# TensorE transposes in place of transposing DMAs for the rounded integers and the one-hot rows, and the second pair of a branch later on VectorE

## The chip, the cores and the metric

The kernel runs on one core of one Trainium2 chip, in one launch. The metric is the device time of an execution in microseconds (us); lower is better. A time given for a kernel is the median of several executions. The profile is one execution of its own, taken by the hardware profiler, and its span is counted from its first to its last instruction.

## The reference

The input x has 2 x 2048 tokens of 512 channels. The first part of the computation (a modulated linear layer, a gated recurrence over the tokens and a gated feed-forward layer) gives a new x; it takes some 1380 us of the kernel and is not touched by the change. The second part is what matters here. With LN for a layer norm with its gains g and offsets b, and with gains and offsets that are looked up per token in a table:

```
h = LN(x; pw_g[pathway], pw_b[pathway])        # 500 classes
h = LN(h; cp_g[comp], cp_b[comp])              # 5 classes
t = LN(x; tm_g[time], tm_b[time])              # 5 classes
s = LN(x; ms_g[scale], ms_b[scale])            # 3 classes
m, n, r = x + one vector per sample (three small networks)
cat = concat(w0*h, w1*t, w2*m, w3*n, w4*r, w5*s)
c = LN(silu(cat @ int_W1 + b1) @ int_W2 + b2; int_g, int_be)
q = clip(round(c / scale_per_token), -127, 127)      # integers
out = x + (q @ q_rhs) * scale_per_token * scale_per_column
```

## The kernel before, in words

**Blocks.** The second part works on eight blocks of 512 tokens (NB = 8). A block holds its tokens as four tiles of 128 (J = 4), which are handled as two pairs (PAIRS). Data stand either by channels (128 channels on the partitions, tokens along the row: x2T, tT, mT, hT) or by tokens (128 tokens on the partitions: x2n, ln, h0, o4).

**The loop.** The loop at line 1800 runs over the blocks. Round i runs `up(i)`, the product with int_W1, and then `down2(i)`, the product with int_W2. `up` calls `paired_in_place` (line 176), which forms a 2 x 2 block product from seven half-size products, called steps 0 to 6 here. Each step is 32 matmuls of 128x128 by 128x256 f32 into one PSUM bank: step 0 into ps_h_a, 1 into ps_h_b, 2 and 3 into ps_h_d, 4 into ps_h_a, 5 into ps_h_e, 6 into ps_h_a. VectorE and ScalarE empty the banks between them: `out11` (L1600), `out12` (L1603, reads ps_h_d), `tap` (L1578 `less`, L1580 `k3`, L1582 the copies), `out22` (L1608), `out21` (L1613). `added` (L1594) adds two matmuls of a table by z2T to a bank; the one into ps_h_d behind step 5 must wait until `out12` has read that bank.

**Work hung into the steps.** The dictionary `then` names what is traced behind a step: key n is behind step n, key (n, u) behind the first or second half of it. In a round with a block before and a block after, the kernel hangs in: the last norm of the block before (0), its rounding to integers (1), the product of the first pair of integers with rhs (2) and of the second (3, 0), the preparation `by_tokens` of the next block (3), `rows_by_tokens` (6, 0) and `branch_by_channels` (6).

**Preparation of the next block.** `norm_by_tokens` (line 1443) turns x2T to tokens on TensorE (tr_x), takes the statistics, and builds z1: for each token its one-hot row times the reciprocal standard deviation, split over several bf16 terms and repeated for four groups of 32. z1 is turned to classes by tokens (z1T) by `to_rows` (line 1437), one transposing DMA on SP's queue. `branch_by_tokens` (line 1479) gathers the 500-class gains and offsets by token with indirect DMAs on POOL's queue into pw0 and pw1, and applies them to pair 0 and pair 1 on VectorE (L1502, L1503): h0. In the profile pw0 is named zone_B and pw1 pw. `rows_by_tokens` (line 1508) takes the statistics of pair 1 and builds z2, which `to_rows` turns to z2T in the same way. `branch_by_channels` turns h0 to hT on TensorE (tr_h). `gains` (line 1540) multiplies the turned rows by the tables of gains on TensorE and by x on VectorE: n = 0 makes tT and n = 1 mT from z1T, n = 2 makes hT from z2T. A call of `gains` issues four matmuls for two banks of the pools `tr`.

**Integers.** `int8_values` (line 1676) rounds a pair (qn, in the places q0 and q1, which z1 and z2 use as well) and turns it by a transposing DMA to qT (L1685). `int8_product` (line 1690) multiplies it by the integers of rhs (ps_f, L1657).

**Buffers.** PSUM has two pools of one buffer each for turned data, `tr_A` and `tr_B`, taken in turn by `tr(...)` (line 1342), and `m2_ps` with four banks for everything else. Some places in SBUF bear the names of zones in the profile: zone_A holds x2T of even blocks, o4_0 and q0; zone_C holds x2n of even blocks, o4_1 and z1T; zone_B holds pw0 and the copies k0 to k2.

**What sets the order.** Each engine runs its instructions in one order, which a planner makes from a priority (the order in which the code is traced), the data dependencies and its own estimates of durations. `tc.issue_after(ins)` queues instructions behind one of the same engine. In block 0 the order of TensorE up to the end of step 1 is written out by hand, and the calls hung in are those of `in_first`: the second part of z2 goes by a DMA there, and the first is turned on TensorE by `rows_of_first`. The last block has no next one and ends in `part_norm` and `part_product`, where the integers are already turned on TensorE (trq, L1725).

Of the kernel before, what the change touches and what calls it, by code (L numbers as in the profile page):

```python
# [10 lines left out]
BF = mybir.dt.bfloat16  # L11
# [6 lines left out]
P = 128  # L18
B, L, D, F = 2, 2048, 512, 1536
C = D // P  # L20
# [30 lines left out]
def adaln_attn_ffn(ctx: ExitStack, tc: tile.TileContext, a: dict, out: bass.AP):  # L51
# [1382 lines left out]
        )  # L1434
        return ins

    def to_rows(dst, src):
        nc.sync.dma_start(
            dst.rearrange("p a (j t) -> p (a j) t", t=P),
            src.rearrange("p a j t -> p (a j t)"), transpose=True,  # L1440
        )

    def norm_by_tokens(i, k, behind=()):


        def queued(n):
            return tc.issue_after(behind[n].ins) if behind else nullcontext()

        x2n = k["x2n"] = place(f"x2n{i % 2}", J, D)
        mv = small.tile([P, J, 2], FP, tag="mv", name=f"mv1_{i}", bufs=4)  # L1450
        for q in PAIRS:
            if behind:
                turn[0] = 1
            with queued(q):
                pt = tr(f"tr_x_{i}_{q}")
                for j in (0, 1):
                    for c in range(C):
                        nc.tensor.transpose(
                            pt[:, j, ts(c, P)], k["x2T"][:, c, ts(2 * q + j, P)], ident
                        )  # L1460
            nc.scalar.copy(duo(x2n, q), pt)
            for j in (2 * q, 2 * q + 1):
                stats(mv, j, x2n[:, j, :], f"s1_{i}")
        r = rstd_of(mv, f"r1_{i}")

        z1 = by_tiles("q0", i)
        rows = as_rows(r, mv, f"w1_{i}")
        spread_in_groups(z1[:, 0], i, slice(0, 5), rows[:, 0])
        ins = spread_in_groups(z1[:, 1], i, slice(5, 8), rows[:, 0])
        k["z1T"] = place("z1T", 2, T, dtype=BF)  # L1470
        to_rows(k["z1T"], z1)

        k["ln"] = [place(f"o4_{q}", 2, D) for q in PAIRS]
        with tc.issue_after(ins.ins):
            for j in range(J):
                normed(k["ln"][j // 2][:, j % 2, :], x2n[:, j, :], mv, r, j)
        k["rows"] = rows

    def branch_by_tokens(i, k):


        ln = k["ln"]
        z2 = by_tiles("q1", i)
        of_means = z2[:, 1, :, 3 * R : NR].rearrange("p j (q r) -> p j q r", r=RB - R)
        nc.scalar.copy(
            z2[:, 1, :, 0 : 3 * R].rearrange("p j (n r) -> p j n r", r=R),
            onehot[:, i * J : i * J + J, :].unsqueeze(2).to_broadcast([P, J, 3, R]),
        )

        h0 = k["h0"] = []  # L1490
        mv2 = small.tile([P, J, 2], FP, tag="mv", name=f"mv2_{i}", bufs=4)

        def pair_stats(q):
            for j in (0, 1):
                stats(mv2, 2 * q + j, h0[q][:, j, :], f"s2_{i}")

        for q in PAIRS:
            pw = place(f"pw{q}", 2, 2 * D)
            h0.append(pw[:, :, 0:D])
            for j in (0, 1):  # L1500
                gather(i * J + 2 * q + j, pw[:, j, :])
            nc.vector.tensor_mul(h0[q], ln[q], h0[q])  # L1502
            nc.vector.tensor_add(h0[q], h0[q], pw[:, :, D : 2 * D])  # L1503
            if not q:
                pair_stats(0)
        k["rest"] = z2, of_means, mv2, pair_stats

    def rows_by_tokens(i, k):
        z2, of_means, mv2, pair_stats = k["rest"]
        rows = k["rows"]  # L1510
        pair_stats(1)
        spread(of_means[:, :, :, 0:8], i, slice(0, 8), rows[:, 1])
        r = rstd_of(mv2, f"r2_{i}")
        rows = as_rows(r, mv2, f"w2_{i}")
        spread_in_groups(z2[:, 0], i, slice(0, 5), rows[:, 0])
        last = spread(of_means[:, :, :, 8:], i, slice(0, 5), rows[:, 1])
        k["z2T"] = place(f"z2T{i % 2}", 2, T, dtype=BF)
        if i:
            to_rows(k["z2T"], z2)
        else:  # L1520
            k["z2"] = z2
            to_rows(k["z2T"][:, 1:2], z2[:, 1:2])
        return last

    def rows_of_first():

        pt = m2_ps.tile([P, D], BF, tag="mm", name="tr_z2")
        for j in range(J):
            nc.tensor.transpose(pt[:, ts(j, P)], k["z2"][:, 0, j, :], identb)
        nc.scalar.copy(k["z2T"][:, 0, :], pt)  # L1530

    def by_tokens(i, k):
        norm_by_tokens(i, k)
# [27 lines left out]
    def up(i, k, then):  # L1561
        h1 = h1s[i] = block("h1")
        h_a, h_b = slice(0, H), slice(H, T)

        first, second = (k["x2T"], block("mT")), (block("tT"), block("hT", i))

        def banks(n):
            return m2_ps.tile([P, 2, H], FP, tag="mm", name=f"ps_h1_{i}_{n}").rearrange(
                "p u t -> u p t"
            )  # L1570

        def both(ps):
            return ps.rearrange("u p t -> p u t")

        def tap(n, ps, less):
            t = place(f"k{ {1: 0, 4: 1, 2: 2, 5: 1, 3: 1, 6: 2}[n]}", 2, H)
            if n == 5:
                nc.vector.tensor_sub(t, ps, less)  # L1578
            elif n == 3:
                held["k3"] = nc.vector.tensor_add(t, both(ps), less)  # L1580
            else:
                nc.scalar.copy(t, both(ps))  # L1582
            return t

        def silu(o, half, src):
            nc.scalar.activation(
                h1[:, o, half], src, AF.Silu, bias=col("L0_cond2_int_b1", o)
            )

        def added(n, ps):  # L1590

            o, half = {1: (0, h_a), 2: (0, h_b), 3: (2, h_b), 4: (2, h_a)}[n]
            for u in (0, 1):
                nc.tensor.matmul(  # L1594
                    ps[u], tables[:NR, 3, ts(o + u, P)], k["z2T"][:NR, 1, half],
                    start=False, stop=(n != 2), skip_group_check=True,
                )

        def out11(ps, kept):
            nc.vector.tensor_add(h1[:, 0:2, h_a], both(ps), kept)  # L1600

        def out12(ps, kept):
            nc.vector.tensor_add(h1[:, 0:2, h_b], both(ps), kept)  # L1603
            for o in (0, 1):
                silu(o, slice(0, T), h1[:, o, :])

        def out22(ps, kept):
            nc.vector.tensor_add(h1[:, 2:4, h_b], both(ps), kept)  # L1608
            for o in (2, 3):
                silu(o, h_b, h1[:, o, h_b])  # L1610

        def out21(ps, kept):
            nc.vector.tensor_add(h1[:, 2:4, h_a], both(ps), kept)  # L1613
            for o in (2, 3):
                silu(o, h_a, h1[:, o, h_a])

        paired_in_place(
            w_int, *([t[:, :, h] for t in q] for h in (h_a, h_b) for q in (first, second)),
            banks, tap, out11, out12, out21, out22, then, added, True, None if i else behind_branch,
        )  # L1620

    def down2(i, nxt):
# [4 lines left out]
        for q in (1, 0):  # L1627
            for j in (2 * q, 2 * q + 1):
# [1 line left out]
                    gains(i + 1, nxt, (2, 3, 0).index(j))  # L1630
                ps = m2_ps.tile([P, D], FP, tag="mm", name=f"ps_o_{i}_{j}")
                for c in range(C):
                    nc.tensor.matmul(  # L1633
                        ps, h1[:, c, ts(j, P)], w2[:, c, :], start=(c == 0), stop=(c == C - 1)
                    )
                t = o4[q][:, j % 2, :]
                nc.vector.tensor_add(t, ps, b2_bc)
                stats(mv, j, t, f"s3_{i}")
# [37 lines left out]
    def int8_values(i, qs, q):  # L1676

        t = o4s[i][q]
        for j in (0, 1):
# [2 lines left out]
        qn = place(f"q{q}", 2, D, dtype=BF)  # L1682
        rounded(qn, t)
        nc.vector.tensor_scalar(qn, qn, -127.0, None, ALU.max)
        nc.sync.dma_start(  # L1685
            place(f"qT{q}", 2, D, dtype=BF).rearrange("p j (c t) -> p (j c) t", t=P),
            qn.rearrange("p j d -> p (j d)"), transpose=True,
        )

    def int8_product(i, qs, x2n, q, behind):  # L1690

# [42 lines left out]
    with tc.high_priority():  # L1734
        k = load(0)
        norm_by_tokens(0, k, (ends[4], mids[5]))
        branch_by_tokens(0, k)
        branch_rows = rows_by_tokens(0, k)

    first_block = ExitStack()  # L1740
# [43 lines left out]
    def behind_branch(n):  # L1784
# [3 lines left out]
    in_first = {  # L1788
        (0, 1, 0): steps(class_bias, lambda: branch_by_channels(0, k)),
        (0, 0, 1): times,  # L1790
        (0, 1, 1): rows_of_first,
        (1, 0, 0): lambda: gains(0, k, 2),
        1: first_block.close,
    }
    def behind_k3(i, k):
        with tc.issue_after(held["k3"].ins):
            rows_by_tokens(i, k)

    last = None
    for i in range(NB):  # L1800
        nxt = load(i + 1) if i + 1 < NB else None
        then = {} if last else in_first
        if last:
            qs = []
            then[0] = lambda: qs.append(last_norm(i - 1))
            then[1] = lambda: [int8_values(i - 1, qs[0], q) for q in PAIRS]
            then[2] = lambda: int8_product(i - 1, qs[0], last["x2n"], 0, held["ins"])
            then[3, 0] = lambda: int8_product(i - 1, qs[0], last["x2n"], 1, held["ins"])
        if nxt:
            then[3] = lambda: by_tokens(i + 1, nxt)  # L1810
            then[6, 0] = lambda: behind_k3(i + 1, nxt)
            then[6] = lambda: branch_by_channels(i + 1, nxt)
        else:

# [83 lines left out]
```

## Time and profile before

| | us |
|---|---|
| median of 3 executions | 1993.96 (1993.28 to 1995.19) |
| the profiled execution | 1991.8 |
| its span | 1990.0 |
| TensorE busy (99%) | 1972.5 |
| VectorE busy (59%) | 1180.4 |
| ScalarE busy (33%) | 658.4 |
| GpSimd busy (7%) | 146.4 |
| mean granted clock of TensorE | 0.997 |

In the profile PE is TensorE's matmuls, PEld its weight loads, DVE is VectorE, ACT is ScalarE, POOL is GpSimd, and SPq is the DMA queue that SyncE issues to. A line such as "DVE h L1603" means the instruction of line 1603 that writes tile h. Matmuls overlap each other, so the time of a group of them is longer than the distance between the starts by the length of one. Transposing DMAs of the span: eight for z1T (named zone_C), eight for z2T, and seven for each qT, all on SP's queue. TensorE has transposes of f32 tiles (tr_x, tr_h) and, in two places, of bf16 tiles: four of z2 in block 0 (tr_z, L1529) and sixteen of integers in the tail (trq, L1725).

### The profile page before, as it was taken

What the parts mean: (1) busy time and instruction counts of PE and PEld (TensorE: products, weight loads), DVE (VectorE), ACT (ScalarE), POOL (GpSimd) and SP (SyncE); (2) the same over time, 40 slices, a digit from 0 to 9 for tenths busy, and PEclk for the clock granted to TensorE, in tenths of its full rate; (3) what the DMA queues carried; (4) which work ended last, traced back from release to release, by engine and by line L of the source; (5) the groups of instructions that cost most, each with busy time, mean ns of one, the idle gap of its engine ahead of it and who ended that gap; (6) DMA issues with size and microseconds to landing.
All of it is one profiled execution on the core that took longest, in us unless ns stands there. A gap on an engine that the chain in (4) does not pass through costs nothing.

```text
span 1990.0 us, 16593 instructions
## 1 busy us (share of the span) xinstructions
PE 1972.5 (99%) x6060; PEld 1054.8 (53%) x6068; DVE 1180.4 (59%) x1907; ACT 658.4 (33%) x889; POOL 146.4 (7%) x123
## 2 busy tenths in 40 slices
PE   9999999999999999999999999999999999999997
PEld 5444444444444444444444444444867867877774
DVE  6667666666633324324224564646788888788775
ACT  4557777777522222222221100001213213212302
POOL 0241000000400000000010000025000000000000
PEclk9999999999999999999999999999999999999999
DMA  6661212121511212111335666453322222222110
GB/s 220 204 201 53 89 59 95 53 95 43 159 47 66 89 42 82 56 42 53 101 100 170 209 232 235 156 170 127 121 69 85 59 72 82 65 73 74 43 32 22
DMA packets 115774, 201.36 MB, mean 101 GB/s; under 512 B 37728, under 2 KB 66034, under 8 KB 111596
## 3 DMA queue, kind: packets, MB, share of 16 engines
q1 hardware_dynamic: 111028, 183.49, 28.2%
q0 software_dynamic: 4608, 16.78, 2.4%
q8 instruction: 48, 0.79, 0.2%
q14 instruction: 34, 0.28, 0.0%
q10 hardware_dynamic: 56, 0.03, 0.0%
HBM read 133.59 MB, written 58.83 MB: 97 GB/s over the span
## 4 chain that ended last, share of the span: by engine, by line
PE 93%; DVE 5%; ACT 0%; DMA 0%; issue 0%; SPq 0%; DVEq 0%
PE up_a L134 17%; PE rec_a L134 11%; PE dn_a L134 8%; PE up_d L134 8%; PE ps_h_a L134 6%; PE ps_h_d L134 6%; PE rec_d L134 6%; PE ps_o L1633 5%; PE dn_d L134 4%; PE up_b L134 4%; PE ps_h_b L134 3%; PE y_a L134 3%; PE rec_b L134 3%; PE dn_b L134 2%; PE y_d L134 1%; PE ps_f L1657 1%
## 5 line engine op out<-in xcount | busy, mean ns | idle before, releaser
L134 PE MATMUL up_a<-h,w_up 128*128 128x512 f32 x384 | 172.6, 592 | 0.0
L134 PE MATMUL dn_a<-op,w_dn 128*128 128x512 f32 x384 | 168.9, 599 | 0.0
L821 DVE SCALAR_TENSOR_TENSOR prod<-up_d,cols,k 128x512 f32<-128x512 f32 x48 | 36.0, 750 | 199.5 <-ACT k L304 199.5
L304 ACT COPY k<-up_a 128x512 f32<-128x512 f32 x144 | 84.0, 584 | 196.8 <-PE up_a L134 196.7
L801 ACT ACTIVATE gate<-gate,cols 128x512 f32<-128x512 f32 x96 | 68.8, 721 | 215.3 <-DVE gate L800 214.2
L134 PE MATMUL up_a<-h2T,w_up 128*128 128x512 f32 x288 | 129.5, 593 | 0.0
L134 PEld LDWEIGHTS up_a<-h,w_up 128*128 128x128 f32 x384 | 73.1, 190 | 91.7 <-issue 89.3
L134 PEld LDWEIGHTS dn_a<-op,w_dn 128*128 128x128 f32 x384 | 73.0, 192 | 90.2 <-issue 89.7
L134 PE MATMUL rec_a<-h,w_rec 128*128 128x512 f32 x256 | 115.1, 592 | 0.0
L134 PE MATMUL rec_a<-hT,w_rec 128*128 128x512 f32 x256 | 115.1, 592 | 0.0
L1633 PE MATMUL ps_o<-int_w,h 128*128 128x512 f32 x224 | 103.6, 606 | 0.0
L134 PEld LDWEIGHTS up_a<-h2T,w_up 128*128 128x128 f32 x288 | 54.8, 190 | 68.8 <-issue 68.8
L134 PE MATMUL up_b<-h,w_up 128*128 128x512 f32 x192 | 86.3, 592 | 0.0
L134 PE MATMUL up_d<-h,w_up 128*128 128x512 f32 x192 | 86.3, 593 | 0.0
L134 PE MATMUL dn_d<-op,w_dn 128*128 128x512 f32 x192 | 83.7, 594 | 0.0
L134 PEld LDWEIGHTS rec_a<-hT,w_rec 128*128 128x128 f32 x256 | 48.7, 190 | 61.2 <-issue 61.2
L134 PEld LDWEIGHTS rec_a<-h,w_rec 128*128 128x128 f32 x256 | 48.7, 190 | 61.2 <-issue 60.7
L304 ACT COPY k<-rec_a 128x512 f32<-128x512 f32 x96 | 55.6, 579 | 71.5 <-PE rec_a L134 70.0
L800 DVE TENSOR_TENSOR gate<-up_b,k 128x512 f32<-128x512 f32 x48 | 32.9, 690 | 72.1 <-PE up_b L134 71.0
L134 PE MATMUL up_d<-h2T,w_up 128*128 128x512 f32 x144 | 65.2, 593 | 0.0
L1633 PEld LDWEIGHTS ps_o<-int_w,h 128*128 128x128 f32 x224 | 40.3, 190 | 46.5 <-issue 46.5
L222 DVE TENSOR_TENSOR op<-op,op 128x3072 f32<-128x3072 f32 x16 | 55.2, 3448 | 16.2 <-PE dn_d L134 9.3
(408 smaller groups left out, 3403.2 us busy)
## 6 DMA issues: line engine op xcount, KB each, us to landing
pp_d<-prod SPq DMA_DIRECT2D x48, 512.0 KB
op<-pp_d SPq DMA_DIRECT2D x16, 1536.0 KB
y_d<-y SPq DMA_DIRECT2D x16, 512.0 KB
h<-y_d SPq DMA_DIRECT2D x4, 2048.0 KB
yr<-y_d SPq DMA_DIRECT2D x16, 512.0 KB
hs_d<-yr SPq DMA_DIRECT2D x16, 512.0 KB
h<-hs_d SPq DMA_DIRECT2D x4, 2048.0 KB
op<-in_xT SPq DMA_DIRECT2D x32, 256.0 KB
```

What stands on the lines that cost most here:

```text
L134: ins = nc.tensor.matmul(ps, ws[k // 2][:, slot, k % 2, ts(u, P)], xs[k], start=(first and k == 0), stop=(last and k == n - 1), skip_group ...
L222: nc.vector.tensor_sub(t, p, q)
L304: nc.scalar.copy(t, ps)
L800: nc.vector.tensor_add(gate[u][:, half], ps, kept)
L801: nc.scalar.activation(gate[u][:, half], gate[u][:, half], AF.Gelu, bias=col("L0_attn_mlp_gate_b", fs[u]),)
L821: nc.vector.scalar_tensor_tensor(prod[u][:, b_], ps, col("L0_attn_mlp_fc_b", fs[u]), kept, ALU.add, ALU.add)
L1633: nc.tensor.matmul(ps, h1[:, c, ts(j, P)], w2[:, c, :], start=(c == 0), stop=(c == C - 1))
L1657: nc.tensor.matmul(ps, qT[:, ts(c, P)], rq[:, c, :], start=(c == 0), stop=(c == C - 1))
```

## The change

z1, z2 and the integers of the blocks 0 to 6 are turned by TensorE, through a bank of `tr` and a copy by ScalarE, and no transposing DMA is left. z1 of the next block is turned behind step 4, z2 behind the matmuls of the third tile (j = 2, the first that `down2` works on), the first pair of integers behind the first half of step 2 and the second behind step 2. In block 0 z2 is turned in two parts through banks of `m2_ps`. The multiplication and addition of pair 1 in `branch_by_tokens` become a function `pair(q)` of their own, which for pair 1 is traced behind step 5 and queued on VectorE behind `less`; in block 0 it is called right after `branch_by_tokens`.

```diff
-    def to_rows(dst, src):
-        nc.sync.dma_start(
-            dst.rearrange("p a (j t) -> p (a j) t", t=P),
-            src.rearrange("p a j t -> p (a j t)"), transpose=True,
-        )
+    def to_rows(dst, src, pt):
+        for n in range(dst.shape[1]):
+            for j in range(J):
+                nc.tensor.transpose(pt[:, n, ts(j, P)], src[:, n, j, :], identb)
+        nc.scalar.copy(dst, pt)
...
-        to_rows(k["z1T"], z1)
+        k["z1"] = z1
...
+        def pair(q):
             nc.vector.tensor_mul(h0[q], ln[q], h0[q])
-            nc.vector.tensor_add(h0[q], h0[q], pw[:, :, D : 2 * D])
-            if not q:
-                pair_stats(0)
+            nc.vector.tensor_add(h0[q], h0[q], place(f"pw{q}", 2, 2 * D)[:, :, D : 2 * D])
+
+        pair(0)
+        pair_stats(0)
+        k["pair"] = pair
...
-        if i:
-            to_rows(k["z2T"], z2)
-        else:
-            k["z2"] = z2
-            to_rows(k["z2T"][:, 1:2], z2[:, 1:2])
+        k["z2"] = z2
...
+    def rows_of_first(n):
+
+        pt = m2_ps.tile([P, 1, D], BF, tag="mm", name=f"tr_z2_0_{n}")
+        to_rows(k["z2T"][:, n : n + 1], k["z2"][:, n : n + 1], pt)
+
+    def rows_of(n, i, k):
+        to_rows(k[f"z{n}T"], k[f"z{n}"], tr(f"tr_z{n}_{i}", BF))
...
-                nc.vector.tensor_sub(t, ps, less)
+                held["less"] = nc.vector.tensor_sub(t, ps, less)
...
+                if nxt and j == 2:
+                    with tc.issue_after(ins.ins):
+                        rows_of(2, i + 1, nxt)
...
-        nc.sync.dma_start(
-            place(f"qT{q}", 2, D, dtype=BF).rearrange("p j (c t) -> p (j c) t", t=P),
-            qn.rearrange("p j d -> p (j d)"), transpose=True,
-        )
+
+    def int8_rows(i, q, behind):
+
+        qn, pt = place(f"q{q}", 2, D, dtype=BF), tr(f"trq_{i}_{q}", BF)
+        with tc.issue_after(behind.ins):
+            for j in (0, 1):
+                for c in range(C):
+                    nc.tensor.transpose(pt[:, j, ts(c, P)], qn[:, j, ts(c, P)], identb)
+        nc.scalar.copy(place(f"qT{q}", 2, D, dtype=BF), pt)
...
         norm_by_tokens(0, k, (ends[4], mids[5]))
+        rows_of(1, 0, k)
         branch_by_tokens(0, k)
+        k["pair"](1)
...
-        (0, 1, 1): rows_of_first,
+        (0, 1, 1): lambda: rows_of_first(0),
+        (1, 1, 0): lambda: rows_of_first(1),
...
-            then[2] = lambda: int8_product(i - 1, qs[0], last["x2n"], 0, held["ins"])
+            then[2, 0] = lambda: int8_rows(i - 1, 0, held["ins"])
+            then[2] = lambda: (
+                int8_rows(i - 1, 1, held["ins"]),
+                int8_product(i - 1, qs[0], last["x2n"], 0, held["ins"]),
+            )
...
-            then[6, 0] = lambda: behind_k3(i + 1, nxt)
+            then[5] = lambda: behind("less", nxt["pair"], 1)
+            then[6, 0] = lambda: behind("k3", rows_by_tokens, i + 1, nxt)
+            then[4] = lambda: behind("ins", rows_of, 1, i + 1, nxt)
```

`behind(name, f, *args)` calls f inside `tc.issue_after(held[name].ins)`.

More of the change, by code (lines that the diff above doesn't have):

```diff
@@ L1517, in rows_by_tokens @@
         k["z2T"] = place(f"z2T{i % 2}", 2, T, dtype=BF)
-        if i:
-            to_rows(k["z2T"], z2)
-        else:
-            k["z2"] = z2
-            to_rows(k["z2T"][:, 1:2], z2[:, 1:2])
-        return last
[L1525 to L1530, printed above, removed]
+        k["z2"] = z2
+        return last
+    def rows_of_first(n):
[3 more added lines that the diff above has]
+        to_rows(k[f"z{n}T"], k[f"z{n}"], tr(f"tr_z{n}_{i}", BF))
     def by_tokens(i, k):
@@ L1632, in down2 @@
                 for c in range(C):
-                    nc.tensor.matmul(
+                    ins = nc.tensor.matmul(
                         ps, h1[:, c, ts(j, P)], w2[:, c, :], start=(c == 0), stop=(c == C - 1)
                     )
+                if nxt and j == 2:
+                    with tc.issue_after(ins.ins):
+                        rows_of(2, i + 1, nxt)
                 t = o4[q][:, j % 2, :]
@@ L1794, in adaln_attn_ffn, with behind @@
     }
-    def behind_k3(i, k):
-        with tc.issue_after(held["k3"].ins):
-            rows_by_tokens(i, k)
+    def behind(name, f, *args):
+        with tc.issue_after(held[name].ins):
+            f(*args)
     last = None
```

## The prediction, made before the changed kernel was run

> **What bounds the kernel now.** I read the page first, then TensorE's waits, then the order of time in one block of the last stage.
>
> From the page (busy us, share of the span):
> ```profile
> span 1990.0 us, 16593 instructions
> PE 1972.5 (99%) x6060; PEld 1054.8 (53%) x6068; DVE 1180.4 (59%) x1907; ACT 658.4 (33%) x889; POOL 146.4 (7%) x123
> ```
> TensorE (PE) works through the whole span; VectorE and ScalarE have room. A busy PE is not always a useful one, so the next question is where it waits. From TensorE's waits (total us, times, longest):
> ```profile
> PE ps_h_d L1594 <- DVE h L1603: 3.6, 7, 0.6
> PE ps_h_b L134 <- DVE tT L1555: 0.9, 1, 0.9
> PE tr_z L1529 <- ACT q L1432: 0.4, 1, 0.4
> ```
> Nowhere in this view does PE wait for a transposing DMA: the waits that are not here lie at the start or in the tail, which the change leaves alone. One wait comes back seven times, once in every block that prepares a next one. Its cause is in VectorE's order of time of such a block (start us, us):
> ```profile
> 1504.65 1.22 DVE L1502 TENSOR_TENSOR zone_B<-zone_A,zone_B 128x1024 f32<-128x1024 f32 x1
> 1505.79 1.22 DVE L1502 TENSOR_TENSOR pw<-zone_C,pw 128x1024 f32<-128x1024 f32 x1
> 1506.92 1.21 DVE L1503 TENSOR_TENSOR zone_B<-zone_B 128x1024 f32<-128x1024 f32 x1
> 1508.06 1.22 DVE L1503 TENSOR_TENSOR pw<-pw 128x1024 f32<-128x1024 f32 x1
> 1509.19 1.28 DVE L1348 BATCH_NORM_STATS2 s_st<-zone_B 128x6 f32<-128x512 f32 x2
> ...
> 1510.47 0.65 DVE L1603 TENSOR_TENSOR h<-ps_h_d,zone_B 128x512 f32<-128x512 f32 x1
> ```
> L1603 is `out12`: it empties the bank ps_h_d, which PE adds to next. Ahead of it stand both pairs of the first branch, zone_B (pair 0) and pw (pair 1). VectorE has idled before this run and is busy without a gap from 1501 on, so its queue, not data, makes L1603 late. PE sees (start us, us, then idle before):
> ```profile
> 1508.78 1.89 PE L134 MATMUL ps_h_e<-mT,w_int 128*128 128x256 f32 x8
> 1511.17 0.38 PE L1594 MATMUL ps_h_d<-z2T,tables 108*128 108x256 bf16 x2 [0.51 <-DVE h L1603]
> ```
> So the block's period, 73.0 us (ps_h_a begins at 1463.30 and 1536.32 on the chain), is PE's work plus 0.5.
>
> **What the change adds: transposes on PE.** The counts are from the code. Per prepared block: 8 for z1, 8 for z2, and, for the integers of the block before, 2 x 8. That is 32 in each of seven rounds (224), and 12 for block 0 (8 of z1, the 4 of z2 that a DMA did). Same operation, same type and shape, back to back, in the tail and once in block 0:
> ```profile
> 1972.83 0.61 PE L1725 MATMUL trq<-identb,zone_B 128*128 128x128 bf16 x8
> 1398.47 0.38 PE L1529 MATMUL tr_z<-identb,q 128*128 128x128 bf16 x4 [0.38 <-ACT q L1432]
> ```
> One lasts 0.219 us, but eight take 0.61: the pitch is (0.61 - 0.22) / 7 = 0.0555 us. PE has nothing idle to hide them in, so they count in full: 224 x 0.0555 = **12.4 us**, and 12 x 0.0555 = **0.7 us** for block 0. Not pipelined they would cost 236 x 0.219 = 51.7 us; the row shows them pipelined, so I take the pitch.
>
> The Trainium skill speaks against the change here: "TensorE: Matmul & The Clock Gate", Part 4, PE-mode transpose, gives about 275 ns for one 128x128 bf16 transpose inside a kernel and 390 ns alone. By that, an estimate from the page, 236 would take 64.9 us and the kernel would come near 2060 us. This trace's pitch of 0.0555 us differs from it five times over, and the measurement decides.
>
> A seam behind them: f32 transposes of the same 128 columns come every 0.109 us (ten from 1495.60, the next matmul at 1496.69), so an f32 weight load seems to need that much, where a 0.055 us transpose before it covers half. Two groups a round are followed by f32 work (the first integers in the middle of step 2, z1 before step 5): 14 x 0.054 = **0.8 us**, bounds nothing and 14 x 0.3 = 4.2 (the seam behind a `gain` group, below).
>
> **ScalarE's copies** cost four of 1024 bf16 columns per round. No row shows one: 0.569 us for 512 bf16 (L1530) and 1.01 us for 1024 f32 (L1374) bound it; I take 1.0, so 4 us more of a 73 us round, in an engine that is busy 33%. Each stands ahead of its user by this order: the first integers turn at about 1480.8 (values rounded at 1478.7), copied by 1482.3, used at 1484.5; z1's last copy of rows ends at 1503.57, and step 4 ends on PE at 1503.6, so its transposes begin without a wait, though with almost no slack; its z1T is used at 1520.4. The copies that empty ps_h_a (1503.86) and ps_h_d (1486.22) share the queue with them. If one such copy were put ahead of an emptying one, PE would wait up to 1 us.
>
> **The two banks `tr`.** z2 turns behind the matmuls of the second half's first tile, at about 1525, in a bank that the next `gains` needs: its second pair now waits for the copy, to about 1526.4. PE's order is made by the planner, which already splits such a group:
> ```profile
> 1520.43 0.39 PE L1551 MATMUL gain<-zone_C,tables 30*128 30x512 bf16 x2
> 1520.76 1.13 PE L1633 MATMUL ps_o<-int_w,h 128*128 128x512 f32 x2
> 1521.81 0.39 PE L1551 MATMUL gain<-zone_C,tables 30*128 30x512 bf16 x2
> 1522.13 2.84 PE L1633 MATMUL ps_o<-int_w,h 128*128 128x512 f32 x6
> 1524.91 0.40 PE L1551 MATMUL gain<-zone_C,tables 18*128 18x512 bf16 x4
> 1525.23 3.70 PE L1633 MATMUL ps_o<-int_w,h 128*128 128x512 f32 x8
> ```
> The first `gains` stands in two groups of 2 because its second bank is still being emptied; the second stands in one of 4. From that group at 1524.91 to the one at 1528.87 are 3.96 us, and eight ps_o at 0.432 (dn_a: 36 in 15.54) make 3.46: a group costs 0.50 us, of 2 or of 4, as the four run side by side. I expect the group of 4 to be split: 7 x 0.50 = **3.5 us** (bounds 0 and a PE that waits in order, 7 x 1.0 = 7).
>
> **What it removes.** With pair 1 behind `less`, the two operations of pair 1 (1.14 each) leave VectorE's queue ahead of L1603, which ends at 1508.9 instead of 1511.1; step 5 now ends at about 1511.1 with z1's 0.44. The 0.51 goes with 2.2 us to spare: **-3.6 us** for seven. Pair 1 then runs from 1509.5 to 1511.8, in VectorE's time before k3 (1511.89), and tr_h reads it only at 1519.2; statistics of pair 1 stay behind k3. What is late next is PE itself. Block 0's own pair keeps its place, and no gather moves on POOL's queue in the loop (each waits for tr_h).
>
> The transposing DMAs leave SP's queue: eight of z1, eight of z2, fourteen of the integers, 1.23 us of issue each. Behind them SP issues the load of x2T (1508.97, which waits for PE) and the outputs, none of which PE waits for. Worth nothing. In block 0, z1's transposes stand in the last matmuls of the stage before (about 1375 to 1383); z1T is read at 1383.70, and the bank is free by then: nothing beyond the 0.44 counted.
>
> **Sum:** 12.4 + 0.7 + 0.8 + 3.5 - 3.6 = **+13.8 us**. The profiled execution took 1991.8 us (span 1990.0 and 1.8 around it), so 2005.6; the median shown is 1993.96, 2.2 above it, and against that I predict **2007.8 us**, 0.7% slower. About 0.2% (4 us) is what a measurement of this kernel can tell from no change.
>
> **Rivals.**
> - *No split* (28%): the second `gains` stays in one group without a wait. The gaps between groups on PE would be as before. +10.3: 2004.3 us.
> - *A new wait* (16%): z1's slack is under 0.2 us, and four more copies stand in ScalarE's queue; one wait of 1 us a round on PE adds 7: 2014.8 us. Against it: ScalarE idles for over 2 us ahead of most of these places.
> - *The wait stays* (8%): if the planner keeps pair 1 ahead of L1603, or the emptying copy of ps_h_a comes late behind z1's, the 3.6 are not gained: 2011.4 us. This is the case that the change does not do what it says.
> - *Not slower* (8%): the groups of `gains` merge. There are four a round at 0.50; if the new order issues two fewer in each of seven rounds, 7.0 come back on top of the case without a split: +3.3, 1997.3 us, within the 4 us. It decides from two merged groups a round on; one alone leaves +6.8. For it: two of the groups are parts of one `gains`. Against: the copies of tr_h that split them are unchanged. A gain beyond that would need PE work that vanishes, and none does.
>
> **How the numbers follow.** The forecast has 40%, the rivals 28, 16, 8 and 8. PE's 13.1 us of transposes are certain within a few tenths, so all but the last are slower by over 0.2%. The low end, 2000.7, is the case without a split, less 0.8 of seams and 2.8 for waits in block 0 and before step 3 that transposes may fill; the high end is 2014.8, the new wait. Outside lie the last rival and part of the new wait. Slower 0.90, within 0.2% 0.06, faster 0.04 (half of the last rival, and all that I overlook).
>
> **What would show it.** In the profile after: 7 waits of ps_h_d for L1603 gone; trq, tr_z1, tr_z2 groups of 8 at 0.055 pitch; the block's period 73.0 + 1.8 = 74.8 us; the second `gains` as 2 + 2; no wait over 0.1 us at a transpose. A pitch near 0.1, or a wait for ScalarE at a `tr` bank or at ps_h_a, would make the prediction too low; a period under 74 us would make it too high.

## The result and the profile after

The changed kernel takes 2007.65 us (median of 4, 2006.97 to 2009.90) beside 1993.62 us of the kernel before: a ratio of 1.0073, with a 95% interval of 1.0056 to 1.0090. It is slower by about 14 us; the forecast was 2007.8 us.

The profiled execution took 2007.17 us, with this head of its page:

```profile
span 2005.4 us, 17000 instructions
PE 1990.9 (99%) x6296; PEld 1069.6 (53%) x6304; DVE 1179.0 (59%) x1907; ACT 687.2 (34%) x919; POOL 146.2 (7%) x123
```

The 236 further matmuls on PE are the transposes. PE is as full as before, at a longer span; VectorE's work is the same, and ScalarE has 29 us more, the copies. The span grew by 15.4 us, of which 1.6 are not the change's: on PE, the last transposes of x ahead of every changed instruction begin 1.56 us later than in the profile before (1368.84 and 1367.28). What is left, 13.8 us, is the change.

TensorE's waits after (total us, times, longest) no longer hold the seven for L1603 (L1604 now). Of block 0's waits one grew from 0.4 to 0.6 and one came twice instead of once:

```profile
PE ps_h_b L134 <- DVE tT L1556: 1.5, 2, 0.9
...
PE tr_z L1440 <- ACT q L1432: 0.6, 1, 0.6
```

VectorE's order of time in the same round (start us, us) shows `out12` (L1604) moved ahead of both the addition of pair 0 and all of pair 1 (pw); it ends at 1511.27, 4.5 us before PE needs its bank at 1515.80:

```profile
1509.44 1.22 DVE L1504 TENSOR_TENSOR zone_B<-zone_A,zone_B 128x1024 f32<-128x1024 f32 x1
1510.58 0.69 DVE L1604 TENSOR_TENSOR h<-ps_h_d,zone_B 128x512 f32<-128x512 f32 x1
...
1514.19 1.19 DVE L1504 TENSOR_TENSOR pw<-zone_C,pw 128x1024 f32<-128x1024 f32 x1
```

And PE's order, with the three kinds of transposes (trq for the integers, tr_z from zone_A for z1, tr_z from q for z2) and the group that broke:

```profile
1484.47 0.61 PE L1696 MATMUL trq<-identb,zone_A 128*128 128x128 bf16 x8
1484.91 1.95 PE L134 MATMUL ps_h_d<-tT,w_int 128*128 128x256 f32 x8
1486.69 1.89 PE L134 MATMUL ps_h_d<-hT,w_int 128*128 128x256 f32 x8
...
1508.39 0.61 PE L1440 MATMUL tr_z<-identb,zone_A 128*128 128x128 bf16 x8
...
1514.07 1.89 PE L134 MATMUL ps_h_e<-mT,w_int 128*128 128x256 f32 x8
1515.80 0.38 PE L1595 MATMUL ps_h_d<-z2T,tables 108*128 108x256 bf16 x2
...
1529.44 0.61 PE L1440 MATMUL tr_z<-identb,q 128*128 128x128 bf16 x8
1529.99 0.39 PE L1552 MATMUL gain<-zone_C,tables 18*128 18x512 bf16 x2
1530.31 1.13 PE L1634 MATMUL ps_o<-int_w,h 128*128 128x512 f32 x2
1531.36 0.39 PE L1552 MATMUL gain<-zone_C,tables 18*128 18x512 bf16 x2
```

Eight transposes begin at 1484.47 and the next matmul at 1484.91: they cost the stream 0.44 us, whatever the 0.61 of their row says. From 1514.07 to 1515.80 are 1.73 us, eight matmuls at 0.216: ps_h_d is waited for no more. The second `gains` (18 rows) stands as 2 + 2 with two matmuls of ps_o between, where it was one group of 4.

A number to compare kernels by is the period: the distance between the starts of step 0 (the first matmul into ps_h_a) in consecutive rounds. Over the six full rounds of a trace (those with a block before and a block after) it repeats within 0.02 us, where medians scatter by 1 us. It was 73.03 us and is 74.78 us, 1.74 more before rounding. The experiments are read by it.

### The profile page after: what moved, and what is told of

It is laid out like the page before. It is cut to its first block, busy times and chain, and to the rows that moved or that the text cites. A ratio compares the mean times of both kernels' runs of the same rounds, so it can differ in the third digit from the quotient of the medians.

```text
span 2005.4 us, 17000 instructions
## 1 busy us (share of the span) xinstructions
PE 1990.9 (99%) x6296; PEld 1069.6 (53%) x6304; DVE 1179.0 (59%) x1907; ACT 687.2 (34%) x919; POOL 146.2 (7%) x123
## 4 chain that ended last, share of the span: by engine, by line
PE 99%; DVE 1%; ACT 0%; issue 0%
PE up_a L134 16%; PE rec_a L134 11%; PE dn_a L134 8%; PE up_d L134 8%; PE ps_h_a L134 8%; PE ps_h_d L134 6%; PE rec_d L134 6%; PE ps_o L1634 5%; PE dn_d L134 4%; PE up_b L134 4%; PE ps_h_e L134 3%; PE y_a L134 3%; PE rec_b L134 3%; PE ps_h_b L134 3%; PE dn_b L134 2%; PE y_d L134 1%
```

## The experiments

The theory behind all of them: the stream of PE is the time. Each term of the sum is a piece of that stream, and nothing off PE counts unless PE waits for it.

**1. Pair 1 alone.** The kernel before, with the one edit:

```diff
+        pair(0)
+        pair_stats(0)
+        k["pair"] = pair
...
+            then[5] = lambda: behind("less", nxt["pair"], 1)
```

> The kernel before with the second pair alone moved: queued on VectorE behind `less`, all transposes by DMA as before. The theory (TensorE's stream of work is the time, and every term of the sum is a piece of it): the seven waits for L1603 go, and each was worth its idle 0.51 us plus the 0.16 by which a matmul's modelled end (0.38 us) lies behind the next start at full pitch (0.216): 7 x 0.67 = -4.7 us, a period of 72.36 us, about 1989 beside 1993.6 us. As the prediction sized it: -3.6, about 1990. Rival (pair 1 only moves the wait to k3 or to tr_h): within 1 us of before.

Measured: 1991.02 us beside 1992.55, ratio 0.9988 (0.9979 to 0.9997); the period is 72.65, so 0.39 us less a round, not 0.67 (and not the 0.51 of the prediction). The wait for L1603 is gone, and a new one of 0.3 stands seven times. PE, then ScalarE, in that round:

```profile
1521.03 0.38 PE L1598 MATMUL ps_h_a<-z2T,tables 108*128 108x256 bf16 x2
1521.70 0.39 PE L1555 MATMUL gain<-zone_C,tables 30*128 30x512 bf16 x2 [0.29 <-ACT hT L1374]
```
```profile
1520.25 0.49 ACT L1432 COPY q<-q 128x360 bf16<-128x360 bf16 x1 [2.48 <-DVE q L1423]
1520.65 1.92 ACT L1374 COPY hT<-tr_h 128x1024 f32<-128x1024 f32 x2
```

ScalarE's queue holds the copy of z2 ahead of the copies of tr_h. PE reaches this place earlier than before, the chain that makes z2 does not, and `gains` finds its bank still full. In the kernel before, the copies of tr_h began with ScalarE waiting for PE:

```profile
1519.37 1.93 ACT L1374 COPY hT<-tr_h 128x1024 f32<-128x1024 f32 x2 [0.17 <-PE tr_h L1371]
```

The rival had the kind right, not the size: 0.28 of the 0.67 came back as a wait for the copies of tr_h.

**2. The transposes without the move.** The changed kernel, with pair 1 back ahead of `out12` (its two later calls go):

```diff
         pair(0)
         pair_stats(0)
-        k["pair"] = pair
+        pair(1)
...
```

> The changed kernel with pair 1 back in its old place ahead of L1603: all transposes on TensorE, nothing moved on VectorE. The theory: z1's transposes put 0.50 us (8 x 0.0555 and a seam of 0.054) between the start of VectorE's chain and the place where TensorE needs ps_h_d, so they lie in the old wait, and only 0.17 of it is left: +1.2 us against the changed kernel, 2008.9. Then most of what the move gains alone is gained by z1's transposes already, and the move itself is worth little in the changed kernel. Rival (the terms add, as the prediction summed them): the whole wait is back, +3.6 to +4.7, 2011.3 to 2012.4 us.

Measured: 2006.87 us beside 1992.55, ratio 1.0071 (1.0057 to 1.0085), which the medians can't tell from the changed kernel's 1.0073. The period can: 74.95, 0.17 above 74.78, as the theory had it. In the changed kernel the move is worth 0.17 us a round and not 0.5.

**3. The integers alone.** The kernel before with `int8_rows` and its two calls in place of the DMA at L1685, nothing else.

> The kernel before with only the integers turned on TensorE; z1 and z2 by DMA, pair 1 in its old place. The theory: seven rounds of 16 transposes at 0.0555 and one seam of 0.054 behind the first group: 7 x 0.94 = +6.6 us, the wait for L1603 unchanged at 0.51, about 2000.2 us. Rival (no split groups of gains in the account, the 13.8 us lie in dearer transposes, about 0.075 us each): 112 x 0.075 = +8.4, about 2002 us. Rival (the waits of the integers on a DMA cost TensorE something): less than +6.

Measured: 2000.14 us beside 1992.55, ratio 1.0035 (1.0022 to 1.0047); period 73.99, +0.96 (expected 0.94). The waits for L1603 stand as they were (3.7 us in 7). Taking fourteen transposing DMAs away gave PE no measurable time back.

**4. z2 through another bank.** The changed kernel, with

```diff
-        to_rows(k[f"z{n}T"], k[f"z{n}"], tr(f"tr_z{n}_{i}", BF))
+        name = f"tr_z{n}_{i}"
+        pt = tr(name, BF) if n == 1 else m2_ps.tile([P, 2, D], BF, tag="mm", name=name)
+        to_rows(k[f"z{n}T"], k[f"z{n}"], pt)
```

> The changed kernel with z2 turned through a bank of m2_ps instead of tr, so that the second gains need not wait for the copy of z2 and stand in one group of four. The theory: seven groups fewer at 0.515 us, -3.6 us against the changed kernel, a period of 74.26 us, about 2004.0. Rival (the time lies in the transposes, and a split group costs nothing): 2007.6, the period as it was at 74.78 us.

Measured: 2003.14 us beside 1992.55, ratio 1.0052 (1.0039 to 1.0066); period 74.26, 0.52 below the changed kernel. PE's order of time shows why:

```profile
1528.09 0.61 PE L1440 MATMUL tr_z<-identb,q 128*128 128x128 bf16 x8
1528.64 0.40 PE L1554 MATMUL gain<-zone_C,tables 18*128 18x512 bf16 x4
1528.96 3.70 PE L1636 MATMUL ps_o<-int_w,h 128*128 128x512 f32 x8
```

The bank was the cause of the split, and a split costs 0.52 us.

**5. The integers twice.** The changed kernel, each transpose of the integers issued twice into the same place (`for j in (0, 0, 1, 1)`).

> The changed kernel with each transpose of the integers issued twice into the same bank (112 more on TensorE, the same values). The theory: a further transpose costs its pitch and nothing else, 16 x 0.0555 = 0.89 us a round: a period of 75.67 us beside 74.78, +6.2 us, about 2013.5. Rival (a transpose costs what a single one lasts, 0.219, or more): +24.5 us and up.

Measured: 2013.98 us beside 1992.84, ratio 1.0106 (1.0090 to 1.0121); period 75.67, +0.89, the expected number. The group of sixteen:

```profile
1484.88 1.06 PE L1696 MATMUL trq<-identb,zone_A 128*128 128x128 bf16 x16
1485.77 1.95 PE L134 MATMUL ps_h_d<-tT,w_int 128*128 128x256 f32 x8
```

Sixteen in 0.89 us of the stream: 0.056 each, also in a longer run. This settles the price of a transpose in a row here. It is the pitch, not the 0.219 that one lasts. For one in a kernel the Trainium skill ("TensorE: Matmul & The Clock Gate", Part 4, PE-mode transpose) gives about 0.275, which the prediction weighed and which is not the price here either.

**6. z1 alone.** The kernel before with z1 turned on TensorE behind step 4; z2, the integers and pair 1 as before.

> The kernel before with only z1 turned on TensorE; z2 and the integers by DMA, pair 1 in its old place. The theory: the 0.50 us of z1's transposes lie in the wait for L1603, so the period stays at 73.03 us and the wait shrinks from a loss of 0.67 to 0.17; only block 0's 0.44 is paid, about +0.4 us. Rival (the terms add): 7 x 0.50 + 0.44 = +3.9 us, a period of 73.53, the wait unchanged.

Measured: 1994.39 us beside 1992.84, ratio 1.0003 (0.9994 to 1.0012), no difference; period 73.04. Eight transposes a round cost nothing here, because they stand where PE waited. PE at `out12`'s bank:

```profile
1509.48 1.89 PE L134 MATMUL ps_h_e<-mT,w_int 128*128 128x256 f32 x8
1511.38 0.38 PE L1603 MATMUL ps_h_d<-z2T,tables 108*128 108x256 bf16 x2
```

From 1509.48 to 1511.38 are 1.90 us for eight matmuls of 0.216 (1.73): 0.17 are lost to a wait, though the row shows no idle time. In the kernel before it was 1511.17 - 1508.78 = 2.39, so 0.66 were lost, where the row says 0.51.

**7 to 9. Toward a faster kernel.** The prices above point at the kernel before: keep the DMAs, drop the wait, and keep the groups whole. First, experiment 1 with the first `gains` behind the second product of ps_o (four matmuls in the profile):

```diff
-                if nxt and j in (2, 3, 0):
+                if nxt and j in (3, 0):
...
+                    if nxt and j == 2 and c == 1:
+                        with tc.issue_after(ins.ins):
+                            gains(i + 1, nxt, 0)
```

> The kernel before with pair 1 moved (as in the first experiment) and the first gains queued behind the second matmul of ps_o, so that both its banks are free and its four matmuls stand in one group. The theory: a group fewer is worth 0.515 us a round, and the new wait of the first experiment (gain for the copy of tr_h, 0.28 us) goes with it, since two matmuls of ps_o stand ahead: a period of 73.03 - 0.67 - 0.515 = 71.85 us, 7 x 1.18 = -8.3 us, about 1985 us. Rival (splitting a group costs nothing, only the wait goes): 72.36, about 1988. Rival (tT comes late for the next block): no better than the first experiment's 72.65.

Measured: 1988.08 us beside 1992.84, ratio 0.9975 (0.9964 to 0.9985); period 72.37, not 71.85. The first `gains` was whole and its wait gone (0.28), but now the second broke:

```profile
1523.16 0.39 PE L1555 MATMUL gain<-zone_C,tables 30*128 30x512 bf16 x4
1523.48 1.98 PE L1637 MATMUL ps_o<-int_w,h 128*128 128x512 f32 x4
1525.40 0.39 PE L1555 MATMUL gain<-zone_C,tables 18*128 18x512 bf16 x2
1526.00 0.39 PE L1555 MATMUL gain<-zone_C,tables 18*128 18x512 bf16 x2 [0.21 <-issue]
```

Between the two calls there are only 1.9 us of ps_o, and VectorE reads the first call's second bank until 1525.95. The theory's number failed. The first rival's number (72.36) was met, but not by its reason: splitting costs, and the split came back elsewhere.

Next, the product of the first integers behind the table matmuls of step 2 (`added`, n = 2), so that PE has work while ScalarE empties ps_h_d:

```diff
+            if n == 2 and "first" in held:
+                held.pop("first")(ins)
...
-            then[2] = lambda: int8_product(i - 1, qs[0], last["x2n"], 0, held["ins"])
+            held["first"] = lambda ins: int8_product(i - 1, qs[0], last["x2n"], 0, ins)
```

> The kernel of the last experiment, and the product of the first pair of integers queued behind the table matmuls of step 2 instead of ahead of them. TensorE then has 1.73 us of work while ScalarE empties ps_h_d (0.58), where now six transposes of x (0.65) leave it 0.285 us short ahead of step 3. The theory: 0.285 us a round less, a period of 71.56 us, about 1983 us. Rival (the integers' product or the transposes of x come late elsewhere, so that the wait turns up again before step 4 or at the norm): the period stays at 71.85 or more.

Measured: 1985.66 us beside 1992.84, ratio 0.9966 (0.9954 to 0.9978); period 72.09, 0.29 below experiment 7, the expected step (0.285) from another start. The product, of whose eight matmuls the profile kept seven, now stands between the two, and step 3 begins eight pitches of 0.216 behind its start, without a loss:

```profile
1481.66 0.38 PE L1598 MATMUL ps_h_d<-z2T,tables 108*128 108x256 bf16 x2
1481.88 1.89 PE L1666 MATMUL ps_f<-rq,qT 128*128 128x512 bf16 x7
1483.61 1.89 PE L134 MATMUL ps_h_d<-x2T,w_int 128*128 128x256 f32 x8
```

Last, all three `gains` behind the second product of their tile:

```diff
-                if nxt and j in (3, 0):
-                    gains(i + 1, nxt, (2, 3, 0).index(j))
...
-                    if nxt and j == 2 and c == 1:
+                    if nxt and j in (2, 3, 0) and c == 1:
                         with tc.issue_after(ins.ins):
-                            gains(i + 1, nxt, 0)
+                            gains(i + 1, nxt, (2, 3, 0).index(j))
```

> The kernel of the last experiment with all three gains of a round queued behind the second product of their tile of ps_o. In the two experiments before, the first gains became whole, but the second then found its second bank still being read by VectorE and broke in two, with a loss of 0.59 us between its halves (1525.246 to 1525.840), so nothing was won by the group. The theory (a group costs about 0.5 us wherever it stands): with 1.8 us of ps_o more between the first and the second, no group breaks, a period of 72.09 - 0.59 = 71.50 us, 7 x 0.59 = 4.1 us less, about 1981.5 us. Rival (VectorE's products of the gains set the pace, and the break moves to the third gains or to the next block's first step): 72.0 or more.

Measured: 1982.88 us beside 1993.05, ratio 0.9949 (0.9936 to 0.9963); period 71.49, as expected. It is the fastest kernel of the study, 10 us under the one before and 25 under the changed one. Its groups are whole:

```profile
1522.43 0.40 PE L1555 MATMUL gain<-zone_C,tables 30*128 30x512 bf16 x4
1522.75 3.70 PE L1637 MATMUL ps_o<-int_w,h 128*128 128x512 f32 x8
1526.38 0.39 PE L1555 MATMUL gain<-zone_C,tables 18*128 18x512 bf16 x4
```

## Why the prediction was right, point by point

The account of the 13.8 us, from the places of PE's matmuls in both traces: block 0's z1 0.50; from block 0's first `gains` to the next step 0, 1.78; six full rounds at 1.743, 10.46; the round without a next block 0.95; the tail 0.13. Against the prediction, us a round:

| term | predicted | measured | from |
|---|---|---|---|
| 32 transposes | 1.78 | 1.78 | 16 more: +0.89 (experiment 5) |
| seams to f32 work | 0.11 | 0.11 | 1486.69 - 1484.91 = 1.78 for eight at 0.216, twice |
| a group more of `gains` | 0.50 | 0.52 | 74.78 - 74.26 (4) |
| the wait for `out12` | -0.52 | -0.67 | 0.50 by z1 alone (6), 0.17 by the move on top (2) |
| sum | 1.87 | 1.74 | periods |

- **PE bounds, and transposes count in full**, except where they fill a wait: shown (3, 5, 6). The transposing DMAs were worth nothing to PE (3, 6). The pitch, not the length of one, is the price.
- **The split group**: shown by name and by size (4).
- **The wait**: the sum was right that it goes; its size and its cause were not. It was undersized, 0.51 for 0.67, because the idle time of a row starts at the modelled end of the matmul before, 0.38 after its start, where a next one could start after 0.216. And it was credited to the move on VectorE. z1's transposes alone fill 0.50 of it, so either may be called free: the move gains 0.39 by itself and 0.17 beside z1's transposes. The prediction saw that step 5 ends 0.44 later and used it only as slack. Terms that act on one wait do not add.
- **Block 0** was undersized. z1 cost 0.50 beside 0.44: a seam of 0.05 to the f32 work behind it was not counted. From the first `gains` on, the terms predicted give 0.22 for the second part of z2 and 0.44 + 0.05 + 0.44 + 0.50 - 0.57 for the next block (0.57 is this block's wait for L1603), 1.08, beside 1.78. PE's rows show what is missing. Before, four matmuls of ps_h_d stood between the two parts of tT:

```profile
1399.77 1.13 PE L134 MATMUL ps_h_b<-tT,w_int 128*128 128x256 f32 x4 [0.92 <-DVE tT L1555]
1400.73 1.03 PE L134 MATMUL ps_h_d<-tT,w_int 128*128 128x256 f32 x4
1401.60 1.03 PE L134 MATMUL ps_h_b<-tT,w_int 128*128 128x256 f32 x4
```

  After, they stand later, and PE waits for tT a second time:

```profile
1401.74 1.13 PE L134 MATMUL ps_h_b<-tT,w_int 128*128 128x256 f32 x4 [0.92 <-DVE tT L1556]
1403.47 1.13 PE L134 MATMUL ps_h_b<-tT,w_int 128*128 128x256 f32 x4 [0.60 <-DVE tT L1556]
```

  From start to start, less four pitches, this wait lost 0.87. The wait at tr_z is 0.26 longer, and a wait at tr_h that cost 0.35 before is gone. The wait for L1603 was worth 0.74 by the starts, 0.17 more than its row says. With some 0.08 of seams these come to 1.77. The other traces tell which turn does what: with z1 alone on PE (6), tr_h and tr_z have changed and the four matmuls stand as before; with the integers alone (3) nothing here has changed; with z2 turned as well (2) the second wait for tT is there. So it comes with z2's turn; why that moves the four matmuls is not shown. The undersized block 0 and the oversized rounds nearly cancel. That the total agrees to 0.1 us is in this part luck: the agreement is better than the account behind it.
- **ScalarE's copies** took 1.01 us each, as assumed, and made PE wait at no transposed tile in a full round. The rivals of a new wait, of a wait that stays and of merged groups did not occur.

## What to carry to other kernels

On an engine that is busy 99% of the span, an operation moved onto it costs its pitch unless it fills a wait, and a transfer taken away gives back only what that engine waited for; look for that wait first. Price a wait by the distance between starts less the pitch, and before adding up gains ask which of them end the same wait. A buffer that is shared for one more use can break a group elsewhere: here that was 0.52 of 1.74 us a round. In the kernel before, whole groups, the moved pair and the later product together took the period from 73.03 to 71.49.

## What the runs showed of the hardware that was not expected

- A row's idle time can be short of the loss, or missing, by the difference between a matmul's shown length and its pitch (0.38 and 0.216: 0.16 us a wait).
- A group of `gains` costs the same 0.5 us of PE's stream with two or with four matmuls. They start 0.003 us apart; the first start of a group to the next ps_o is 0.315 us for either size, and the steps of ps_o beside it are 0.525 ahead and 0.533 behind, where 0.429 is their pitch.
- The first matmuls of an execution run at half pace (0.213 us between starts instead of 0.111 for the same ones) for a time that differs between executions. The shown granted clock is 1.00 in both cases: in one stretch (us from the span's start; PE busy, matmuls in brackets) of the kernel before and then of the changed one, in code that the change leaves alone,

```profile
6.00:13.00 7.00, 6.84 (x45) 4.56 (x45) 4.20 (x12) 2.42 (x5) 0.00 (x0) 1.00 1.03 374
```
```profile
6.00:13.00 7.00, 7.00 (x34) 7.00 (x35) 4.12 (x12) 2.30 (x4) 0.00 (x0) 1.00 1.04 382
```

  This put the changed kernel 3.4 us behind. Of that, the kernel before lost 1.7 again in a stretch of lower granted clock near 1134 us (0.59 from 1132 to 1136). Over all eleven profiles the first matmul into y_a begins between 9.6 and 13.2 us. Such differences are as large as some of the effects here, so single profiles are compared by periods and not by spans.
